# A four-layer graph network on one core: layer 3 counts neighbours block by block, with the later blocks' counts as a row of the masks

## The chip, the cores and the metric

The kernel runs on one core of a Trainium2 chip. Five engines work side by side, each on its own queue of instructions: TensorE (PE: matmuls, with PEld for the weight loads), VectorE (DVE), ScalarE (ACT), GpSimd (POOL) and SyncE (SP, which here only issues DMAs). The metric is the device time of one execution in microseconds (us); lower is better.

## What is computed

Four graph layers follow each other over the same adjacency matrix `adj` (3327 x 3327 float32) and node features `x` (3327 x 64). Each layer's output is added to its input and normalised by row. The change concerns layers 2 and 3.

```python
def _L2_gnn_ref(user_embs, adj, W):
    x = user_embs
    for k in range(2):                     
        agg = adj @ x
        x = jnp.tanh(jnp.concatenate([agg, x], axis=1) @ W[k])
    return x

def _L3_gnn_ref(input, adj, weight, bias):
    support = input @ weight
    mask = (adj != 0).astype(support.dtype)
    rank = jnp.cumsum(mask, axis=1)
    deg = rank[:, -1:]
    k = jnp.minimum(deg, float(MAX_NEIGH))   # MAX_NEIGH = 100, DECAY = 0.5
    pos = rank - (deg - k)
    w = mask * jnp.where(pos > 0, DECAY ** (k - pos), 0.0)
    out = w @ support + bias
    return out
```

So in layer 3 the weight of a neighbour j of a node i is a power of one half whose exponent is the number of i's neighbours after j, and it is zero from the hundredth on. What has to be counted for every pair (i, j) is how many entries of row i of `adj` behind column j are not zero.

## The kernel before

`adj` lies transposed in HBM, padded to 3328 x 3328, so a *block* `jb` is 128 source nodes j (on partitions) by all 3328 target nodes i (on the free axis): 1664 KB of float32. There are 26 blocks. The target nodes are worked in two halves of 1664 (`HALF`), and each half in chunks of 416 (`CW`), four to a half.

**Layer 2** runs in `layers`. For each of two hops (`k`), PE multiplies every block's 128 x 3328 values, in float32, with the 64 features of its nodes: `add(c, jb)` does chunk `c` of both halves at once, each half in 64 output columns (line 421). Hop 1 is `k = 0`, hop 2 is `k = 1`. Seven blocks stay in SBUF throughout (`kept`: four "early" ones, 25 to 22, and three "late" ones, 21 to 19). The others are streamed through buffers: four of the pool `strm` (`UNDER_WAY`) and `MORE` = 2 of the pool `more`, with DMAs issued by SP (line 212) as soon as a buffer is free. The blocks that were streamed last in hop 1 are the first of hop 2 (`ready`). The order of blocks is written out in `order`; the blocks in `end` come last, chunk by chunk (`chunk_end`), each chunk followed by a tanh on ACT.

**Layer 3** works in 52 *steps* `q`: two halves `h`, and in each the blocks from the last to the first. For a step, `masks(q)` loads the half block in float32 (line 339; nothing to load for a kept block) and DVE makes a bf16 mask of zeros and ones from it (line 341). Two PSUM tiles `cnt[0]` and `cnt[1]`, 832 target nodes each, hold the running counts. `count(c, tri, q)` (line 526) adds, by a triangular 128 x 128 matrix `tri`, 100 steps of 128 for the entry itself and minus 128 for each later neighbour in the block; when a step is done, `count(c, rest, q)` adds what `tri` left out, so that the counts of whole blocks stay in PSUM for the following, earlier blocks. `advance(c, q)` does both: `rest` for step q, `tri` for q + 1. `read(c, q, vector)` clamps the counts at zero and writes them as 16-bit integers, whose bits, taken as bf16, are the powers of one half: on ACT (line 541) or DVE (line 539). In the main loop half 0 is read by ACT, half 1 by DVE. `products(q, c)` then multiplies these weights with the features, split in three bf16 parts: two parts in one full-width matmul (line 722), three steps (`LEAD`) behind; the third is collected over `GROUP` = 9 steps and done in one run of half-width matmuls (line 737). The loop over `q` at the end of `layers` writes the order of PE by hand: products of step q - 3, then `advance`, for c = 0 and 1. PE is in program order throughout, as DVE and ACT are in layers 2 and 3. Between the halves (`half_out`) and at the end (`last_out`) the sums are added to the input, normalised and stored.

`with_step` is a list of small operations that are done one per step at the loop's beginning: the bf16 parts of the features of the later groups of nodes.

## Time and profile before

| | |
|---|---|
| runs | 552.27, 552.3, 554.47 us; median 552.3 |
| the profiled execution, its own span | 552.8 us |
| hop 1 of layer 2 | 239.5 to 315.4 us |
| hop 2 of layer 2 | 315.4 to 388.7 us, its last chunks run on into the turn |
| turn from layer 2 to layer 3 | to 407.1 us |
| layer 3's loop | to about 536.7 us |
| last sums, normalisation and stores | to 552.8 us |
| `rest` matmuls | 200, 0.176 us from one to the next |
| `tri` matmuls | 208 |
| DMA in all | 143.56 MB, 260 GB/s over the span |

A profile line of a group names the source line, the engine, the operation, what it writes and reads, the shape and the number of instructions; then its busy time, the mean of one in ns, and the engine's idle time before it with what ended it. A line of the timeline gives start and length in us; successive instructions of one kind are merged, so "0.52 ... x2" are two matmuls that together took 0.52 us from the first's start to the second's end. A matmul's recorded time contains its way through the array, so the distance from one start to the next is the cost of one in a row of them. A float32 matmul appears as two records.

### The profile page before, as it was taken

To read this page: it belongs to the slowest core of one execution; us is meant where nothing else is said; L and a number is where in the kernel's file an instruction comes from. 1 tells how busy PE (TensorE), PEld (TensorE's weight loads), DVE (VectorE), ACT (ScalarE), POOL (GpSimd) and SP (SyncE) were. 2 spreads that over 40 slices of the span, in tenths; PEclk is the share of its full clock that TensorE was granted. 3 is DMA by queue.
4 is the path that set the end of the run, shared out by engine and by line. 5 is a ranking of instruction groups with operands and counts; after the bars stand their busy time and mean duration, and the time that the engine had idled before them with its cause. 6 is when DMAs were issued, how large, how long until landed. Compare 5 with 4: busy or idle time off the path is not lost.

```text
span 552.8 us, 7387 instructions
## 1 busy us (share of the span) xinstructions
PE 524.6 (95%) x2841; PEld 228.6 (41%) x2841; DVE 373.2 (68%) x553; ACT 275.2 (50%) x321; POOL 207.6 (38%) x85
## 2 busy tenths in 40 slices
PE   8879999999999999999999999999999999989991
PEld 5622222222222222854444444444455555645551
DVE  6789999999999999899000011200679769697733
ACT  4699999999999997620000100000365333433321
POOL 3599999999999999000000000000001000000000
PEclk9799999999999999899999999999999999999996
DMA  8979667666777626699999049999019994799601
GB/s 288 341 225 301 219 224 234 212 233 208 232 240 225 209 95 277 247 427 427 421 430 395 3 167 422 429 420 383 32 53 362 323 375 140 238 295 354 244 1 37
DMA packets 33892, 143.56 MB, mean 260 GB/s; under 512 B 10269, under 2 KB 11959, under 8 KB 28855
## 3 DMA queue, kind: packets, MB, share of 16 engines
q1 hardware_dynamic: 31511, 142.40, 69.9%
q10 hardware_dynamic: 2336, 0.59, 0.5%
q8 instruction: 24, 0.39, 0.3%
q14 instruction: 21, 0.17, 0.1%
HBM read 141.53 MB, written 0.87 MB: 258 GB/s over the span
## 4 chain that ended last, share of the span: by engine, by line
PE 66%; DVE 16%; ACT 11%; issue 5%; DVEq 0%; POOL 0%; ACTq 0%; POOLq 0%
PE cnt L421 26%; PE cnt L526 11%; DVE v L1124 8%; PE pq L1103 7%; PE acc L722 6%; ACT pq L1116 5%; ACT sg L1076 5%; PE acc L1133 4%; PE acc L737 3%; DVE a L1115 2%; DVE w L539 1%; DVE mask L341 1%; PE cnt L412 1%; PE idle L928 1%; PE pm L1416 1%
## 5 line engine op out<-in xcount | busy, mean ns | idle before, releaser
L1088 POOL TENSOR_TENSOR sg<-sg,at 128x1664 f32<-128x1664 f32 x44 | 163.9, 3751 | 2.0 <-ACT sg L1076 1.9
L1103 PE MATMUL pq<-riT,ljT 64*128 64x416 f32 x416 | 100.8, 561 | 10.3 <-DVE v L1124 6.2
L1116 ACT ACTIVATE pq<-pq,al,ga 128x832 f32<-128x832 f32 x104 | 104.7, 1011 | 11.0 <-DVE a L1115 11.0
L1124 DVE SCALAR_TENSOR_TENSOR v<-pq,a 128x832 f32<-128x832 f32 x104 | 105.4, 1014 | 3.6 <-ACT pq L1116 2.5
L1115 DVE SCALAR_TENSOR_TENSOR a<-pq,sg 128x832 f32<-128x832 f32 x104 | 105.2, 1012 | 0.5 <-PE prep_fours L1194 0.5
L1133 PE MATMUL acc<-v,xv 128*64 128x416 f32 x416 | 95.3, 537 | 0.0
L1076 ACT ACTIVATE sg<-lb,rb 128x1664 f32<-128x1664 f32 (+1 forms) x53 | 87.2, 1647 | 0.0
L541 ACT ACTIVATE w<-cnt 128x832 int16<-128x832 f32 x55 | 47.2, 862 | 71.2 <-PE cnt L526 71.1
L421 PE MATMUL cnt<-at_l,lj 128*64 128x416 f32 x448 | 80.3, 513 | 0.0
L653 POOL TENSOR_TENSOR s<-sq,s 128x384 bf16<-128x384 f32 (+1 forms) x4 | 4.1, 1024 | 197.9 <-ACT s L652 197.9
L506 ACT ACTIVATE x<-cnt 128x416 f32<-128x416 f32 x8 | 4.1, 517 | 130.6 <-PE cnt L421 130.6
L1103 PEld LDWEIGHTS pq<-riT,ljT 64*128 64x128 f32 x416 | 31.3, 184 | 83.7 <-DVE v L1124 82.8
L539 DVE TENSOR_SCALAR w<-cnt 128x832 int16<-128x832 f32 x49 | 50.1, 1022 | 21.2 <-PE cnt L526 20.8
L526 PE MATMUL cnt<-mask,rest 128*128 128x416 bf16 x200 | 51.5, 339 | 2.4 <-ACT w L541 1.4
L526 PE MATMUL cnt<-mask,tri 128*128 128x416 bf16 x208 | 53.5, 339 | 0.1
L722 PE MATMUL acc<-w,s 128*128 128x416 bf16 x208 | 52.5, 339 | 0.5 <-DVE hid L794 0.5
L421 PEld LDWEIGHTS cnt<-at_l,lj 128*64 128x64 f32 x448 | 31.9, 137 | 46.1 <-issue 45.2
L1133 PEld LDWEIGHTS acc<-v,xv 128*64 128x64 f32 x416 | 20.6, 134 | 61.7 <-issue 58.0
L341 DVE TENSOR_SCALAR mask<-ah 128x1664 bf16<-128x1664 f32 x42 | 43.5, 1035 | 1.0 <-DMA ah<-in_adjT 1.0
L409 DVE COPY lj<-pn_l 128x512 f32<-128x512 f32 (+1 forms) x4 | 2.4, 592 | 60.8 <-PE pn_l L373 60.8
L421 PE MATMUL cnt<-kept,lj 128*64 128x416 f32 x224 | 41.2, 513 | 0.0
L1088 POOL TENSOR_TENSOR sg<-sg,kept 128x1664 f32<-128x1664 f32 (+1 forms) x10 | 30.0, 3026 | 0.8 <-ACT sg L1076 0.8
(291 smaller groups left out, 413.8 us busy)
## 6 DMA issues: line engine op xcount, KB each, us to landing
at_l<-in_adjT SPq DMA_DIRECT2D x24, 1664.0 KB, 12.2
at<-in_adjT SPq DMA_DIRECT2D x44, 832.0 KB, 5.0
ah<-in_adjT SPq DMA_DIRECT2D x42, 832.0 KB, 6.5
bt_l<-in_adjT SPq DMA_DIRECT2D x8, 1664.0 KB, 16.7
kept<-in_adjT SPq DMA_DIRECT2D x7, 1664.0 KB, 9.2
lb<-lf_rows SPq DMA_DIRECT2D x2, 384.0 KB, 6.3
ljT<-ljT SPq DMA_DIRECT2D x4, 128.0 KB, 2.3
x<-in_x ACTq DMA_DIRECT2D x1, 416.0 KB, 5.4
```

The costliest lines, as they stand in the source:

```text
L341: nc.vector.tensor_scalar(mask[q], at, 0.0, None, ALU.not_equal)
L421: nc.tensor.matmul(acc[c][h * D : (h + 1) * D, :], hw[:, slot(jb), :], blocks[jb][:, o : o + CW], start=c not in begun, stop=last, skip_gr ...
L526: nc.tensor.matmul(cnt[c][:, e, :], mat, mask[q][:, of], start=start, stop=(mat is tri), skip_group_check=True,)
L539: nc.vector.tensor_scalar(w.bitcast(I16), cnt[c], 0.0, None, ALU.max)
L722: nc.tensor.matmul(acc[h, c][:, e, :], s12[:, slot(jb)].rearrange("p t d -> p (t d)"), ws[q, c][:, e, :], start=first, stop=last,)
L1076: nc.scalar.activation(sg[:, :, of], lbs[:, :, of], AF.Sigmoid, bias=rb[:, sl : sl + 1])
L1088: nc.gpsimd.tensor_tensor(sg[:, :, of], sg[:, :, of], at[:, :, of], ALU.mult)
L1103: nc.tensor.matmul(pq[:, h, :], ljT[h != jb // NBH][rows, of], riT[rows, ch * CW : (ch + 1) * CW], start=True, stop=True,)
L1115: stt(a_s[t], pqs[t], CUBIC_PLUS, us.pop(t), op0=ALU.add, op1=ALU.mult)
L1116: nc.scalar.activation(pqs[t], pqs[t], AF.Square, bias=al[:, one], scale=ga[:, one])
L1124: stt(w, pqs.pop(t), CUBIC_REST, a_s.pop(t), op0=ALU.add, op1=ALU.mult)
L1133: nc.tensor.matmul(accs[cp, ci][h * D : (h + 1) * D, :], xv[:, slot(jb), :], w[:, h, :], start=(jb == orders[cp][0]), stop=(jb == orders[c ...
```

## The change

Layer 3 no longer carries its counts in PSUM from block to block. Instead the counts of all later blocks are made beforehand, in layer 2: for every block, in bf16 masks of zeros and ones, matmuls against a 128 x 32 matrix of ones and zeros (`upto`) add the block's column sums to the rows of all blocks up to it (`t_masks`, `t_counts`); the four chunks of a half go to four groups of 32 output partitions of one PSUM bank. Nineteen blocks are counted in hop 1, the seven others in hop 2. The result is clamped at 127, and goes to a DRAM tensor `t_rows` of one row per block. In layer 3 each mask's row 0 is overwritten, by a DMA, with the row of its block, and row 0 of `tri` becomes minus 128 throughout, so that one `tri` matmul gives the whole count and `rest` disappears. The first node of each block, whose row was taken, is weighted apart (`first_masks`, `first_weights`), and its products come from `first_rows` and `first_products`.

Nine blocks' masks for layer 3 (`resident`: 25 to 17) are made in hop 2, over the full width, and kept as bf16 where the float32 blocks were; the other 17 blocks are loaded again in both halves. In hop 2 the early kept blocks alternate with the ready ones, and the other kept ones come last. `MORE` goes from 2 to 1, `GROUP` from 9 to 7, and the reads of half 1 go to DVE in odd steps and to ACT in even ones. POOL is put in program order too.

```diff
-MORE = 2
+MORE = 1
+CLAMP = 127.0
+FIRST_T = 8
+BATCH_T = 2
+MASKS = 6
+LOADS = 4
-GROUP = 9
+GROUP = 7
...
+    nc.gpsimd.memset(tri[:1, :], -STEP)
...
-        nc.gpsimd.tensor_copy(tri, tri_f)
-        nc.gpsimd.tensor_scalar(rest, tri_f, -1.0, -STEP, ALU.mult, ALU.add)
...
+        upto = carry.tile([P, 64], BF16, name="upto")
+        nc.gpsimd.memset(upto[:, :32], 1.0)
+        nc.gpsimd.memset(upto[:, 32:], 0.0)
+        tb = carry.tile([P, 2, CW], BF16, name="tb")
+        over = carry.tile([P, NP], BF16, name="over")
+        t_rows = dram.tile([NB + 1, NP], BF16, name="t_rows")
...
+        def first_row(keep):
+            while len(no_row) > keep:
+                q = no_row.pop(0)
+                h, jb = steps[q]
+                half = slice(h * HALF, (h + 1) * HALF)
+                nc.scalar.dma_start(mask[q][:1, :], t_rows[jb + 1 : jb + 2, half])
+        def both_masks(jb, at):
+            nc.vector.tensor_scalar(at, blocks[jb], 0.0, None, ALU.not_equal)
+            resident[jb] = at
...
         def masks(q):
             mask[q] = l3m.tile([P, HALF], BF16, tag="mask", name=f"mask_{h}_{jb}")
-            nc.vector.tensor_scalar(mask[q], at, 0.0, None, ALU.not_equal)
+            nc.vector.tensor_scalar(mask[q], ahead.pop(q), 0.0, None, ALU.not_equal)
+            no_row.append(q)
+            load()
...
+        def t_masks(jb):
+            t_done.add(jb)
+            for h, of in enumerate(halves_of(blocks[jb])):
+                m = t_at.pop(0)
+                t_at.append(m)
+                nc.vector.tensor_scalar(m, of, 0.0, None, ALU.not_equal)
+                t_made.append((jb, h, m))
+        def t_counts():
+            while t_made:
+                jb, h, m = t_made.pop(0)
+                for c in range(CPH):
+                    nc.tensor.matmul(
+                        t_ps[h][c * 32 : (c + 1) * 32, :], upto[:, 31 - jb : 63 - jb],
+                        m[:, c * CW : (c + 1) * CW], start=(h, c) not in t_begun,
+                        stop=len(t_done) == NB, skip_group_check=True,
+                    )
+                    t_begun.add((h, c))
+        def t_out():
+            for h in range(2):
+                nc.vector.tensor_scalar(tb[:, h], t_ps[h], CLAMP, None, ALU.min)
+            for c in range(CPH):
+                nc.gpsimd.dma_start(by_chunk(t_rows)[c], tb[c * 32 : c * 32 + NB + 1])
...
+        def first_weights(m0):
+            nc.vector.tensor_scalar(m0, m0, 0.0, (NEIGH + 1) * STEP, ALU.not_equal, ALU.mult)
+            nc.vector.scalar_tensor_tensor(m0, tb, -STEP, m0, op0=ALU.mult, op1=ALU.add)
+            nc.vector.tensor_scalar(tb.bitcast(I16), m0, 0.0, None, ALU.max)
...
                 if k:
-                    order, others, share = order + others[:5], others[5:], 3
+                    end = [jb for jb in kept if jb not in soon]
+                    for i, jb in enumerate(soon):
+                        order.insert(2 * i + 1, jb)
+                    order += others
+                    place = {
+                        0: [(soon[0], over)],
+                        1: list(zip(soon[1:3], slots_of(soon[0]))),
+                        3: list(zip((soon[3], end[0]), slots_of(soon[1]))),
+                        6: [(order[6], slots_of(soon[2])[0])],
+                        7: list(zip(end[1:], slots_of(soon[3]))),
+                        8: [(order[8], slots_of(soon[2])[1])],
+                    }
...
+                    if jb not in t_done and (k or i >= FIRST_T):
+                        t_masks(jb)
+                        if len(t_made) == len(t_at) or len(t_done) == NB:
+                            t_counts()
+                    if k:
+                        for b, at in place.get(i, ()):
+                            both_masks(b, at)
...
+                    if k and i == 8 + len(t_left):
+                        t_out()
+                        for b, at in resident.items():
+                            nc.gpsimd.dma_start(at[:1, :], t_rows[b + 1 : b + 2, :])
...
+                last_t = [jb for jb in kept if jb not in t_done]
+                for i, jb in enumerate(last_t):
+                    t_masks(jb)
+                    if i % BATCH_T == BATCH_T - 1 and jb != last_t[-1]:
+                        t_counts()
                 for c in range(CPH):
                     chunk_end(c)
+                t_counts()
...
-        def count(c, mat, q, start):
+        def count(c, q):
...
-                    cnt[c][:, e, :], mat, mask[q][:, of], start=start,
-                    stop=(mat is tri), skip_group_check=True,
+                    cnt[c][:, e, :], tri, mask[q][:, of], start=True, stop=True,
+                    skip_group_check=True,
...
-            first = steps[q + 1][1] == NB - 1
-            if not first:
-                count(c, rest, q, False)
-            count(c, tri, q + 1, first)
+            count(c, q + 1)
...
+            if c and jb == 6:
+                first_products(h)
...
+        def first_rows():
+            with nc.allow_non_contiguous_dma(reason="one row of each block"):
+                for cg in range(CPH):
+                    e = cg % 2
+                    for h in range(2):
+                        at = slice(cg * 32 + h * NBH, cg * 32 + (h + 1) * NBH)
+                        nc.gpsimd.dma_start(
+                            sf[at, 0, :], s12[:1, h::2].rearrange("p n t d -> p n (t d)")
+                        )
+                        nc.gpsimd.dma_start(sf[at, 1, e * D : (e + 1) * D], s3[:1, h::2])
+        def first_products(h):
+            for part in range(2):
+                for cg in range(CPH):
+                    of = slice(cg * 32, (cg + 1) * 32)
+                    nc.tensor.matmul(
+                        acc[h, cg // 2][:, cg % 2, :], sf[of, part], tb[of, h],
+                        start=False, stop=False,
+                    )
...
-            lambda: other_parts(C), lambda: first_part(E), lambda: rest_of(E),
-            lambda: other_parts(E), lambda: x3_later(C), lambda: x3_later(E),
+            lambda: (other_parts(C), firsts_weighted()), lambda: first_part(E), lambda: rest_of(E),
+            lambda: (other_parts(E), first_rows()), lambda: x3_later(C), lambda: x3_later(E),
...
+            first_row(1 if to_mask else 0)
             read(0, q, False)
...
-            read(1, q, True)
+            read(1, q, q % 2 == 1)
...
-            masks(q + AHEAD)
+            while consumed and consumed[0] <= q:
+                consumed.pop(0)
+            if to_mask and len(consumed) - len(to_mask) + (m0 is not None) < MASKS:
+                masks(to_mask.pop(0))
```

## The prediction

> **What bounds the kernel now.** I read the page's engine totals first, then the chain of waits, then a table of stages, and last the timelines of the two stages that the change touches.
>
> ```profile
> PE 524.6 (95%) x2841; PEld 228.6 (41%) x2841; DVE 373.2 (68%) x553; ACT 275.2 (50%) x321; POOL 207.6 (38%) x85
> PE cnt L421 26%; PE cnt L526 11%; DVE v L1124 8%; PE pq L1103 7%; PE acc L722 6%; ACT pq L1116 5%; ACT sg L1076 5%; PE acc L1133 4%; PE acc L737 3%; DVE a L1115 2%; DVE w L539 1%; DVE mask L341 1%; PE cnt L412 1%; PE idle L928 1%; PE pm L1416 1%
> ...
> 239.50:315.40 75.90, 75.90 (x426) 31.12 (x425) 21.67 (x43) 1.75 (x4) 0.00 (x0) 1.00 0.85 357
> 315.40:388.70 73.30, 73.30 (x418) 31.51 (x418) 8.16 (x10) 0.52 (x1) 0.00 (x0) 1.00 0.85 349
> 388.70:407.10 18.40, 17.33 (x86) 9.15 (x83) 12.61 (x43) 10.43 (x18) 1.12 (x1) 1.00 0.00 1
> 407.10:536.70 129.60, 127.11 (x812) 70.17 (x811) 100.58 (x113) 48.14 (x61) 2.98 (x3) 1.00 0.71 254
> ```
>
> The last four lines are hop 1 of layer 2, hop 2, the turn to layer 3, and layer 3's loop: length, then busy PE, PEld, DVE, ACT, POOL, the clock, the DMA share, GB/s. PE is busy throughout in three of them. So in these stages a PE instruction taken away is worth its spacing until another wait is longer, and one added costs its spacing at once; DVE and ACT have room. Inside the loop:
>
> ```profile
> 498.58 0.52 PE L722 MATMUL acc<-w,s 128*128 128x416 bf16 x2
> 499.03 3.36 PE L737 MATMUL acc<-w,s 128*64 128x416 bf16 x36
> 502.32 0.53 PE L526 MATMUL cnt<-mask,rest 128*128 128x416 bf16 x2
> 502.68 0.52 PE L526 MATMUL cnt<-mask,tri 128*128 128x416 bf16 x2
> 503.03 0.52 PE L722 MATMUL acc<-w,s 128*128 128x416 bf16 x2
> ...
> 404.62 0.51 PE L526 MATMUL cnt<-mask,rest 128*128 128x416 bf16 x2 [0.25 <-ACT w L541]
> ...
> 412.09 0.51 PE L526 MATMUL cnt<-mask,rest 128*128 128x416 bf16 x2 [0.17 <-DVE w L539]
> ```
>
> A pair of bf16 matmuls is followed by the next after 0.352 us (0.176 each) and is over after 0.52. A step is twice (rest, tri, product): 12 x 0.176 = 2.11 us. Every nine steps come 36 half-width matmuls (L737) in 3.29 us, 0.091 each: two column halves at once. The last two lines show the other limit: PE waiting for the read of its counts, 0.05 us after ACT (0.86 us) or DVE (1.02 us) ends.
>
> Hop 2 streams 13 blocks of 1.70 MB; these are the DMA queue's waits (who, for whom, total, times, longest) and one stretch of the stage table:
>
> ```profile
> SPq L212 <- PE cnt L421: 66.3, 13, 26.9
> ...
> 354.00:360.00 6.00, 6.00 (x36) 2.44 (x34) 0.00 (x0) 0.00 (x0) 0.00 (x0) 1.00 1.01 426
> ```
>
> Every load waits for PE to free a buffer, and then runs at 426 GB/s: 4.0 us a block against 2.79 us of PE. From the first issue (324.43) to the one visible stall (PE weights at 372.3, eleventh block) are 47.9 us: 11 x 4.0 plus some 2 us from issue to landing and 2 us of gaps. So DMA already just keeps up.
>
> **What the Trainium skill says.** "TensorEngine Tiling (Array Packing)", Tiling Modes: with 32 output columns four tiles run independently, and a change of mode drains the array. The trace has the half-width case only: 0.091 us each, and 0.10 us lost at 499.03 on entering it. "TensorE: Matmul & The Clock Gate", Part 3, gives 3.07x for four row tiles and 2.38x for three column tiles. "DMA: Bandwidth & Descriptors", Issuing engines are not separate DMA queues: issuing from another engine saves sequencer time only; the trace shows 0.44 to 0.6 us per issue on SP. "SBUF — State Buffer", SBUF: two separate sides: a DMA issued from GpSimd is held up while VectorE runs a two-port operation; this trace has no such DMA.
>
> **The change part by part.**
>
> *1. Layer 3 loses the `rest` matmuls.* 200 x 0.176 = 35.2 us of PE, of which about 48 steps x 0.704 lie in the loop. What is late next is the loop of count and read: a count's result after 0.52, 0.04 to the reader, 0.86 (ACT) or 1.02 (DVE), 0.05 back: 1.47 or 1.63 us. PE alone needs 8 x 0.176 = 1.41. Half 0 of the counts is always read by ACT, half 1 by DVE in odd steps, so steps alternate at 1.47 and 1.63, mean 1.55; after each burst of L737 (now 28 in 2.56 us, every seven steps) one step runs at 1.41. Saved: 48 x (2.11 - 1.55) = 27 us, plus 0.5: **-27.5 us**. ACT then does three reads of 0.76 (spacing) in two steps, 2.3 of 3.1 us; DVE a read and two masks, 2.9 of 3.1: both fit. Loads fall from 42 to 34 half blocks, 2.0 us each, and run ten ahead: no bound.
>
> *2. Additions in that loop.* Sixteen first-row products: 0.7 us (four row tiles) to 2.8 (one by one): 1.5. `first_weights` puts three DVE operations over 128x832, some 3 us by L539's row, into step 6, ahead of the read of step 7; ACT in steps 3 to 9 also has the casts (0.5 us each). Together +2.4, from 0 to 5. ACT issues 34 row DMAs. At 0.5 us each that is 17 us of ACT's queue; if ACT can issue while it computes, it falls into its waits and costs nothing, which I take; if not, steps on which ACT reads both halves are longer by 0.35: about +7. The row has some 6 us from its issue to its count (three steps), against 2.3 to 5.6 us to landing of small transfers on the page. Sum of part 2: **+3.9**.
>
> *3. The turn.* Two or three `rest` pairs of 0.35 us go from a chain alternating with ACT reads (403 to 407): **-0.9**.
>
> *4. Later blocks' counts in hop 1.* 19 of 26 blocks, two halves each: 38 groups of four 32-column matmuls. Bounds of a group: 0.18 us (all four at once, as the pair of L737) and 0.37 (eight instructions, weights and matmul, at L737's 46 ns each; whether that is PE's limit the trace doesn't say). With the page's 3.07x it would be 0.23. I take 0.19: 7.2 us, plus ten entries into the mode at 0.1: 8.2. DVE makes the masks beside it (idle from 262 to 316, 0.95 us each, four per pair of blocks against 5.6 us of PE): nothing. But at the hop's end blocks 25 and 21 follow directly on the pair before: their four masks (3.8 us) can start only when that pair's counts free the buffers, and PE has nothing else: stall 2.8. **+11.0.**
>
> *5. Hop 2.* From its start (315.4) block order[0] is done after 9.4 us. Before: 22 blocks x 2.79, then three at the end, 8.4: 79.2. After, five blocks are ready, alternating with the early ones, so a stream buffer comes free every 5.6 us instead of 2.8, and there are 14 blocks to load with five buffers. Loads of others 0 to 3 go out at 9, 15, 21 and 26 us. DVE now makes the resident masks, 1.9 us per block: those of 21 and 19 wait for block 22's end (29.0), so 18's is made at 32.8 to 34.7 and only then is its buffer free for block 4. From there loads are back to back: block 4 lands at 40.7, block 13 at 40.7 + 9 x 4.0 = 76.7, and PE ends at 76.7 + 2.8 + 8.4 = 87.9. PE alone (79.2, 14 groups with seven entries 3.4, and 2 us waiting for block 0's masks) would end at 84.6; the loads decide. **+8.5**, from 4 to 13. MORE = 1 costs nothing in hop 1: DMA there ends at 303, 12 us before PE.
>
> *6. POOL's DMAs* (counts out and back, first rows): nothing near waits for them except the first-row products, about 25 us after their 16 issues. Below nothing is excluded, above up to 5 us; I take 0. Fewer constants before layer 2: 0.
>
> Sum: -27.5 + 3.9 - 0.9 + 11.0 + 8.5 = -5.0 from the profiled 552.8: 547.8. The runs' median, 552.3, is 0.5 lower: **547.3**.
>
> **Rivals.**
> *A, slower: the 32-column matmuls don't go four at a time.* Place: PE in both hops. At 0.37 a group, 52 x 0.18 = 9.4 more: 556.7. For it: no 32-column matmul in the trace, and 46 ns an instruction is the fastest there. Against: nothing shows that to be a limit. From 0.28 a group on the change no longer pays.
> *B: ACT's row DMAs block it* (or rows land late): +7, 554.5; the loop's period is then 1.75 instead of 1.55. For it: 0.5 us an issue; against: ACT idles 71.1 us for L526.
> *C: the hop hides more*, loads keep up and no DVE work delays them: -4, and part 2 free, -2.4: 541.
> *D: the change doesn't shorten the step*, because the reads pace it already: part 1 gone, 574.8. L539's 0.15 us waits for PE at every step (its row: 20.8 us idle for PE in all) speak against it.
>
> **How the numbers follow.** Forecast 0.50, with its own range 543 to 551.5; A 0.13, B 0.16, C 0.12, A with B or D 0.09. About 0.5% (2.8 us: below 549.5, above 555.1) is what can be told from no change. Faster: 0.44 of the forecast and C: 0.56. Same: 0.06 of the forecast and half of B: 0.14. Slower: A, half of B and the rest: 0.30. The range takes in C's edge, B and A: 541 to 557.
>
> **What would show it.** No `rest` row, 208 `tri` matmuls, PE waiting for ACT and DVE `w` in each step at a spacing of 1.5 to 1.6 us; the loop near 106 us. A row of 128*32 matmuls with 208 records at under 0.05 us each; a gap of about 3 us before hop 1's last chunks; hop 2 with PE waits for loads of its last two blocks. Wrong if groups take over 0.28 us, if ACT shows DMA issues between its reads with PE waiting, or if PE stands in the first-row products.

## The result and the profile after

The changed kernel takes 558.6 us (median of nine runs, 556.9 to 562.8) beside 553.0 us for the kernel before, a ratio of 1.011 with a 95% interval of 1.008 to 1.014. It is slower by 1.1%; the forecast was 547.3 us and faster. Its profiled execution has a span of 556.9 us, against 552.8.

The page of the changed kernel, with the engine totals and the chain of work that ended last, by engine and by line:

```profile
PE 509.1 (91%) x2865; PEld 209.5 (38%) x2865; DVE 404.1 (73%) x577; ACT 293.6 (53%) x345; POOL 229.6 (41%) x121
PE 17%; DMA 7%; DVE 7%; issue 2%; ACT 2%; DVEq 0%; ACTq 0%
PE cnt L515 6%; DMA ah<-in_adjT 4%; PE cnt L646 4%; DMA at_l<-in_adjT 3%; PE acc L868 3%; PE acc L851 3%; DVE w L659 2%; DVE mask L372 1%; ACT w L661 1%; PE both L722 1%; PE t L452 1%; PE cnt L913 0%; DVE sq L755 0%; DVE tm L445 0%; DVE kept L362 0%
```

PE did lose work (524.6 to 509.1 us busy), yet the span grew. The second line shows DMA in the chain, which had no share in it before. (The chain is followed back over a part of the span only, so the shares don't sum to 100%.) Two loads stand in the third line: `at_l` belongs to hop 2, `ah` to layer 3.

The stages of the changed kernel (length, then busy PE, PEld, DVE, ACT, POOL, granted clock, DMA share, GB/s): hop 1, hop 2, turn, loop.

```profile
237.00:324.90 87.90, 85.57 (x577) 33.75 (x576) 58.11 (x81) 2.09 (x6) 0.19 (x2) 1.00 0.73 309
324.90:413.45 88.55, 80.92 (x486) 32.17 (x482) 34.18 (x30) 0.71 (x2) 10.50 (x19) 1.00 0.74 288
413.45:429.70 16.25, 13.97 (x66) 7.61 (x65) 11.80 (x42) 9.74 (x17) 1.09 (x1) 1.00 0.36 147
429.70:543.30 113.60, 101.62 (x652) 52.14 (x652) 69.68 (x80) 67.61 (x85) 14.95 (x19) 1.00 0.62 231
```

For a fair comparison both kernels are cut at the same events on PE: hop 1 begins with its first product of a block, hop 2 with its first `pn_l` matmul, the turn with the first `both`, the loop with the first `acc`, the end with the last `center` products.

| stage | before, us | after, us | difference | forecast |
|---|---|---|---|---|
| hop 1 | 75.92 | 87.90 | +12.0 | +11.0 |
| hop 2 | 75.28 | 88.55 | +13.3 | +8.5 |
| turn | 16.50 | 16.25 | -0.3 | -0.9 |
| loop | 131.40 | 113.60 | -17.8 | -23.6 |
| end | 14.25 | 13.54 | -0.7 | 0 |

They sum to +6.5. (The prediction's table of stages ends them elsewhere: 73.3 us for hop 2 before and 129.6 for the loop.) The part ahead of hop 1, whose code did not change, was 2.4 us shorter in this one execution, so the spans differ by 4.1; hop 1 began between 237.0 and 239.9 us in all the executions below. The two hops gave away 25.3 us and the loop brought 17.8. The forecast was near in hop 1, and off by 4.8 us in hop 2 and by 5.8 us in the loop.

**Hop 1.** The timeline of PE in the changed kernel (start, us, line, what it writes and reads, shape, count, and in brackets the idle time before it with what ended it), first one batch of counts, then the hop's end:

```profile
265.30 3.01 PE L515 MATMUL cnt<-at_l,lj 128*64 128x416 f32 x16
268.25 0.54 PE L452 MATMUL t<-tm,upto 128*32 128x416 bf16 x8
268.61 0.52 PE L452 MATMUL t<-over,upto 128*32 128x416 bf16 x8
269.06 1.27 PE L515 MATMUL cnt<-at_l,lj 128*64 128x416 f32 x6
...
315.62 0.36 PE L452 MATMUL t<-tm,upto 128*32 128x416 bf16 x4 [0.60 <-DVE tm L445]
316.56 0.36 PE L452 MATMUL t<-tm,upto 128*32 128x416 bf16 x4 [0.57 <-DVE tm L445]
317.49 0.36 PE L452 MATMUL t<-over,upto 128*32 128x416 bf16 x4 [0.58 <-DVE over L445]
318.43 0.36 PE L452 MATMUL t<-over,upto 128*32 128x416 bf16 x4 [0.57 <-DVE over L445]
318.72 5.81 PE L515 MATMUL cnt<-kept,lj 128*64 128x416 f32 x32
```

From 268.25 to 269.06, 16 matmuls with 32 output columns take 0.81 us: 0.36 us for eight, so 0.18 us for a group of four. The section Tiling Modes of the Trainium skill's "TensorEngine Tiling (Array Packing)" has four independent tiles for 32 output columns, and this trace agrees: four take as long as one full-width matmul (0.176 us), and don't go one after the other. At the end PE does a group, waits 0.6 us for the next mask, and so on four times: 2.3 us of waits.

**Hop 2.** PE's timeline at its end, and the stage table of the same stretch:

```profile
388.79 3.01 PE L515 MATMUL cnt<-at_l,lj 128*64 128x416 f32 x16 [0.25 <-DMA at_l<-in_adjT]
393.20 3.01 PE L515 MATMUL cnt<-bt_l,lj 128*64 128x416 f32 x16 [1.40 <-DMA bt_l<-in_adjT]
397.19 3.01 PE L515 MATMUL cnt<-at_l,lj 128*64 128x416 f32 x16 [0.98 <-DMA at_l<-in_adjT]
401.44 3.01 PE L515 MATMUL cnt<-at_l,lj 128*64 128x416 f32 x16 [1.24 <-DMA at_l<-in_adjT]
406.34 3.01 PE L515 MATMUL cnt<-at_l,lj 128*64 128x416 f32 x16 [1.89 <-DMA at_l<-in_adjT]
```

```profile
396.00:400.00 4.00, 3.02 (x18) 1.06 (x16) 0.00 (x0) 0.00 (x0) 3.76 (x8) 1.00 1.01 427
400.00:404.00 4.00, 2.77 (x18) 1.06 (x16) 0.00 (x0) 0.00 (x0) 1.92 (x3) 1.00 0.74 258
404.00:408.00 4.00, 2.11 (x14) 0.77 (x12) 0.00 (x0) 0.00 (x0) 2.06 (x4) 1.00 0.36 100
```

The last five blocks are each waited for. The bracket is only the wait that the profile puts down to the load; from one start to the next are 4.0 to 4.9 us, against 2.8 us of matmuls. The DMA engines are full until 400 us and tail off after it.

**The loop.** Two steps in the steady part, by PE's timeline:

```profile
509.34 0.51 PE L646 MATMUL cnt<-mask,tri 128*128 128x416 bf16 x2
...
510.81 0.51 PE L646 MATMUL cnt<-mask,tri 128*128 128x416 bf16 x2
...
512.50 0.51 PE L646 MATMUL cnt<-mask,tri 128*128 128x416 bf16 x2
...
515.67 0.51 PE L646 MATMUL cnt<-mask,tri 128*128 128x416 bf16 x2
```

From 509.34 to 512.50 and on to 515.67 are two steps each: 3.16 us, so 1.58 a step, against the forecast's 1.55. The steady step is not where the time went. The waits in the loop (who, for whom, us in all, times, longest) tell more:

```profile
ACT w L661 <- DVE mask L372: 11.9, 7, 2.8
...
DVE mask L372 <- DMA ah<-in_adjT: 6.5, 5, 2.4
PE cnt L646 <- DVE w L659: 5.6, 6, 2.3
PE cnt L646 <- ACT w L661: 4.6, 8, 1.4
```

Read upwards from the second: a mask waits for its load, ACT stands behind that mask because the row DMA that ACT has to issue needs it, and PE waits for the reads of both engines. The loads are late in the first half above all. When the loop began, four half blocks had been asked for, and SP asked for the fifth 3.0 us into the loop, when a mask had freed its buffer. Two windows of 6 us, one ahead of the loop and one in its first half:

```profile
424.00:430.00 6.00, 4.29 (x20) 2.47 (x20) 3.83 (x14) 4.54 (x8) 0.00 (x0) 1.00 0.00 0
...
454.00:460.00 6.00, 4.54 (x25) 2.22 (x23) 4.47 (x5) 4.07 (x5) 4.32 (x7) 1.00 1.01 400
```

The DMA engines first stand still and then are full (share 0.00 and 1.01), which the loop's mean share, 0.62, hides.

If one takes 0.176 us for each full-width matmul, 0.091 for each half-width one and 0.0575 for each of the 16 first-row products, and leaves out the normalisation's products between the halves, the gaps that remain between PE's instructions are 5.5 us in the loop of the kernel before and 19.9 in this one. The 190 `rest` matmuls of the loop were 33.4 us of PE; 14.4 us of them came back as gaps.

### The profile page after: what moved, and what is told of

Its sections match the earlier page's. It is cut to its first block, busy times and chain, and to the rows that moved or that the text cites. A ratio compares the mean times of both kernels' runs of the same rounds, so it can differ in the third digit from the quotient of the medians.

```text
span 556.9 us, 7703 instructions
## 1 busy us (share of the span) xinstructions
PE 509.1 (91%) x2865; PEld 209.5 (38%) x2865; DVE 404.1 (73%) x577; ACT 293.6 (53%) x345; POOL 229.6 (41%) x121
## 5 line engine op out<-in xcount | busy, mean ns | idle before, releaser
L1287 DVE SCALAR_TENSOR_TENSOR v<-pq,a 128x832 f32<-128x832 f32 x104 | 105.4, 1014 | 3.2 <-ACT pq L1279 2.2
L515 PE MATMUL cnt<-at_l,lj 128*64 128x416 f32 x496 | 91.4, 515 | 4.3 <-DMA at_l<-in_adjT 4.3
L661 ACT ACTIVATE w<-cnt 128x832 int16<-128x832 f32 x79 | 65.9, 864 | 36.9 <-PE cnt L646 24.2
L464 POOL DMA_DIRECT2D t_rows<-tb x4 | 2.6, 711 | 146.7 <-DVE tb L462 146.7
L515 PEld LDWEIGHTS cnt<-at_l,lj 128*64 128x64 f32 x496 | 34.3, 137 | 55.7 <-issue 48.1
L372 DVE TENSOR_SCALAR mask<-ah 128x1664 bf16<-128x1664 f32 x34 | 35.5, 1057 | 11.0 <-DMA ah<-in_adjT 6.5
L659 DVE TENSOR_SCALAR w<-cnt 128x832 int16<-128x832 f32 x25 | 25.5, 1020 | 20.3 <-PE cnt L646 20.3
L646 PE MATMUL cnt<-mask,tri 128*128 128x416 bf16 x136 | 35.0, 338 | 5.4 <-DVE w L659 2.8
L646 PEld LDWEIGHTS <-tri 128*128 128x128 bf16 x208 | 19.7, 97 | 36.3 <-issue 21.6
L445 DVE TENSOR_SCALAR tm<-at_l 128x1664 bf16<-128x1664 f32 x16 | 15.7, 1023 | 16.8 <-PE t L452 16.8
```

The costliest lines, as they stand in the source:

```text
L372: nc.vector.tensor_scalar(mask[q], ahead.pop(q), 0.0, None, ALU.not_equal)
L515: nc.tensor.matmul(acc[c][h * D : (h + 1) * D, :], hw[:, slot(jb), :], blocks[jb][:, o : o + CW], start=c not in begun, stop=last, skip_gr ...
L646: nc.tensor.matmul(cnt[c][:, e, :], tri, mask[q][:, of], start=True, stop=True, skip_group_check=True,)
L661: nc.scalar.activation(w.bitcast(I16), cnt[c], AF.Relu)
L1287: stt(w, pqs.pop(t), CUBIC_REST, a_s.pop(t), op0=ALU.add, op1=ALU.mult)
```

## The experiments

Each kernel is the changed one with the edit shown, but for `no_rest`. Ratios are against the kernel before, timed on the same chip (medians there 553.6 to 554.9 us), with a 95% interval in brackets. Stage lengths are those of one profiled execution each, cut as above.

One thing in these executions is no part of any edit. In some of them the trace shows PE's granted clock at one half for 3.4 us, behind one or more waits of PE. Where the loop's code and data were those of the changed kernel, it took 113.6 us (the changed kernel) and 113.2 us (`hop1`) without such a stretch, 114.8 and 114.7 us with one (`mask18`, `counts_one`), and 116.3 us with two (`late_pool`). So a difference of over half a microsecond between two loops can be read only after a look at the clock. The executions of the stage table above, before and after, have no such stretch in a stage up to the loop's end.

### Hop 2: what makes the loads late

**late_pool**: counts out to HBM, and back into row 0, at the last streamed block instead of the sixteenth position.

```diff
-                    if k and i == 8 + len(t_left):
+                    if k and i == len(order) - 1:
```

> The later blocks' counts are clamped, written out and read back at the last streamed block of hop 2 instead of seven blocks earlier. Theory 'shared DMA engines': GpSimd's small transfers hold up the tail of the last streamed blocks, so PE's five waits for loads at hop 2's end (6.6 us) shrink to about 2.5 us and the kernel gains 3 to 4 us on the changed one, unless the rows then come too late for layer 3's first count (then the gain reappears as a wait at the turn). Rival 'late start': the waits come only from block 4's load starting 35 us into the hop and 4.0 us a block, so nothing changes (within 1 us).

Measured: ratio 1.010 [1.006, 1.014]. Hop 2 stays at 88.5 us with the same waits for loads, 4.3 and 1.4 us. So GpSimd's small DMAs do not slow the loads. The loop took 116.3 us, with two stretches at half clock; the second alone puts PE 1.5 us further behind the changed kernel's loop.

**mask18**: block 18's resident mask beside 17's, so that DVE makes it before those of blocks 21 and 19.

```diff
-                        6: [(order[6], slots_of(soon[2])[0])],
+                        6: list(zip((order[6], order[8]), slots_of(soon[2]))),
-                        8: [(order[8], slots_of(soon[2])[1])],
```

> Block 18's resident mask is made right after 17's (step 6 of hop 2's order) instead of after those of 21 and 19. Theory 'late start': its stream buffer comes free 2.9 us sooner, block 4 is asked for 3 us sooner, all later loads move up, PE's wait for block 0's masks shrinks from 1.8 us to under 0.5: gain 3 us. Rival 'shared DMA engines': the tail is set by GpSimd's transfers, which move up as well: gain 0 to 1 us at the hop's end.

Ratio 1.008 [1.005, 1.012]; hop 2 takes 85.3 us, 3.3 less. The load that waited for that mask starts earlier, and all behind it come earlier. PE still waits 4.4 us for loads.

**early_loads**: the five ready blocks first, then the four kept ones. Two late streamed blocks, 9 and 10, are kept as masks in place of 17 and 18, and the masks of 19 to 21 are made later.

```diff
-                    for i, jb in enumerate(soon):
-                        order.insert(2 * i + 1, jb)
-                    order += others
+                    order += soon + others
...
```

> Hop 2 takes the five blocks that are in their buffers first and the four kept ones after them, so that a buffer comes free with each 2.8 us of PE rather than each second one; the masks of the two streamed blocks that were kept (17 and 18) are replaced by those of two late ones, so no buffer is held by a mask. Theory (late load starts are hop 2's loss, forecast at 2.5 us and measured at 6.6): hop 2 takes 81 to 83 us for 88.5, and PE waits for loads no more than 2 us in all; the loop stays within 1 us. Rival (the DMA's rate of 4.0 us a block sets the hop, whenever the loads start): hop 2 stays above 85, where the version with 18's mask made earlier came out.

Ratio 1.003 [1.001, 1.005]; hop 2 takes 84.9 us, less gain than expected. A stretch at half clock has part in it: from the start of the last streamed block to the hop's end are 8.8 us here and 7.1 in the changed kernel, so that about 83.2 us would be the order's own (an estimate). PE still waited 0.97 and 1.94 us for the last two loads: the loads started early, filled all five buffers, and then none could start until PE had gone through four kept blocks.

**spread**: two of the kept blocks after the ready ones, one after the sixth and one after the ninth streamed block.

```diff
-                    order += soon + others
+                    order += soon[:2] + others[:6] + soon[2:3] + others[6:9] + soon[3:] + others[9:]
```

> As early_loads, but of the four kept blocks only two follow the five ready ones; the other two stand after the sixth and the ninth streamed block, so that the later loads are not asked for only when PE has gone through all four. Theory (early_loads lost 2.9 us to the last two loads because the DMA engines idled from about 354 to 360 us, all buffers full): hop 2 takes 81.5 to 82.5 us, no wait for a load over 0.5 us. Rival (the loads run at 4.0 us a block against PE's 3.0 to 3.4, so the last ones are late in any order): hop 2 stays above 84.

Ratio 1.000 [0.998, 1.002]; hop 2 takes 81.3 us, 7.3 less than in the changed kernel. All that PE waits for in hop 2 is now (the view of waits, PE alone):

```profile
PE t L452 <- DVE tm L445: 1.5, 2, 0.9
```

No load is in it. The rate of the DMA engines was thus no bound; when the buffers came free was. Two things free them sooner here: the order, and that blocks 17 and 18 no longer hold a buffer until their masks are made. `mask18`, which frees block 18's buffer sooner and changes nothing else, had 3.3 of the 7.3 us; how the rest splits was not tried. The rest of hop 2's price against the kernel before, 6.0 us, is mostly the counts' own: 14 groups with seven entries, 3.2 us by hop 1's figures, and this wait of 1.5; the other 1.3 us were not traced.

### Hop 1: what the counts cost

**counts_one**: only the first block's counts are done; the masks are still made.

```diff
-                for c in range(CPH):
+                for c in range(CPH if (h, CPH - 1) not in t_begun else 0):
                     nc.tensor.matmul(
...
```

> Left out: the count matmuls of all blocks but the first; their masks are still made, at the same places and in the same buffers. It prices the matmuls with their waits. Theory (matmuls and the wait for the last masks make hop 1's 12 us): hop 1 falls from 87.9 to 77.5 to 78.5 us, 36 groups at 0.18, nine entries at 0.09 and 2.3 of waits. Rival (the masks on DVE hold the blocks, so the loads come later, and that is what hop 1 pays): hop 1 stays above 83. In hop 2 theory (loads decide) expects no more than 1.5 us off 88.5, though 14 groups and their entries are 3 us of PE; the rival (PE decides there) expects the whole 3 us.

Ratio 0.994 [0.991, 0.996]. Hop 1 takes 76.5 us, 0.6 above the kernel before: the matmuls and the waits for their masks are the whole of its 12 us, and DVE's masks beside PE are free, as forecast. Hop 2 stays at 89.0 us although 3 us of PE's work are gone from it. PE then waits longer for loads there, 9.7 us: the loads decided.

**hop1**: the last counts go behind the third of the four closing chunks, and block 19's masks are made there.

```diff
-                    t_masks(jb)
-                    if i % BATCH_T == BATCH_T - 1 and jb != last_t[-1]:
-                        t_counts()
+                    if jb != last_t[-1]:
+                        t_masks(jb)
                 for c in range(CPH):
                     chunk_end(c)
+                    if c == CPH - 2:
+                        t_counts()
+                        t_masks(last_t[-1])
                 t_counts()
```

> Hop 1 makes its last counts later: those of blocks 25 and 21 go behind the third of the four last chunks, and block 19's masks are made there, so that DVE has some 3 us of PE's own work to make them in. Theory (PE waited for the masks, because DVE starts them only when the last adds are nearly done): the four waits of 2.3 us go and hop 1 takes 85.5 to 86.0 us for 87.9; the whole 0.3 to 0.4% less than the changed kernel. Rival (the masks are late wherever they are put, the wait moves to the end of the last chunk): hop 1 stays within 0.5 us of 87.9.

Ratio 1.007 [1.005, 1.009]; hop 1 takes 85.1 us, 2.8 less. PE's timeline of that version at the hop's end:

```profile
315.33 0.54 PE L452 MATMUL t<-tm,upto 128*32 128x416 bf16 x8
315.69 0.53 PE L452 MATMUL t<-over,upto 128*32 128x416 bf16 x8
316.15 4.41 PE L515 MATMUL cnt<-kept,lj 128*64 128x416 f32 x24
320.49 0.53 PE L452 MATMUL t<-tm,upto 128*32 128x416 bf16 x8
```

The same counts, no bracket: DVE makes the masks while PE does 12 float32 matmuls of its own (24 records).

### The loop: where 5.8 us are

**no_rest**: the kernel before, without the `rest` products, and with the second read in turn by ACT and DVE.

```diff
-            if not first:
-                count(c, rest, q, False)
-            count(c, tri, q + 1, first)
+            count(c, tri, q + 1, True)
...
-            read(1, q, True)
+            read(1, q, q % 2 == 1)
```

> The kernel before, without the second count product of each step and with the second read in turn by ACT and DVE, as in the changed kernel; nothing else of the change. Left out with the product: what later blocks add to a block's counts. It prices the forecast's first term alone. Theory (the term itself was nearly right): the loop takes 104 to 106 us for 131.4, the span 525 to 527. Rival (steps without the product wait more than forecast, and the loop's 5.8 us are lost here): the loop takes 108 us or more.

Ratio 0.968 [0.966, 0.971]. The loop takes 112.6 us, so this comes out on the rival's side: taking `rest` away is worth 18.8 us here and not 27.5. (A stretch at half clock, 68.5 us into this loop, is at most 1.7 of them, 3.4 us at half; with it taken off, 110.9 us, the side is the same.) DVE's timeline in this version shows why:

```profile
437.32 1.03 DVE L341 TENSOR_SCALAR mask<-ah 128x1664 bf16<-128x1664 f32 x1 [1.01 <-DMA ah<-in_adjT]
438.26 1.02 DVE L539 TENSOR_SCALAR w<-cnt 128x832 int16<-128x832 f32 x1
439.34 1.03 DVE L341 TENSOR_SCALAR mask<-ah 128x1664 bf16<-128x1664 f32 x1
441.36 1.03 DVE L341 TENSOR_SCALAR mask<-ah 128x1664 bf16<-128x1664 f32 x1 [0.99 <-DMA ah<-in_adjT]
```

The masks start at intervals of 2.02 us, the time of one half block's load, and each read stands behind a mask that stands behind its load. Steps had become shorter than loads. This version loads 42 half blocks, the changed kernel 34, so it does not give the changed kernel's own share; the next five do.

**same_loads**: layer 3's loads after the first four are left out, and the masks are made from the four buffers that are there.

```diff
+                if len(loaded) == LOADS:
+                    ahead[q] = loaded[q % LOADS]
+                    return
...
+                loaded.append(ahead[q])
```

> Left out: all loads of half blocks in layer 3 after the first four; every later mask is made from those four tiles, so DMA is nearly idle in the loop and no mask waits for a load. Theory 'loads bound the loop': the loop (113.6 us in the changed kernel) falls by 5 to 6 us, no wait of VectorE for a load and no wait of ScalarE for a mask is left. Rival 'row transfers': the loop is held by ScalarE's issues of 34 rows or by their landing, then it falls by less than 2 us.

**rows_none**: the 34 row DMAs are left out.

```diff
-                nc.scalar.dma_start(mask[q][:1, :], t_rows[jb + 1 : jb + 2, half])
```

> Left out: the 34 one-row transfers into the masks (the masks keep their own row 0). Theory 'loads bound the loop': VectorE still waits for loads, but ScalarE no longer stands behind them: gain 1.5 to 3 us. Rival 'row transfers': gain 5 us or more. If ScalarE's issue costs nothing and the loads alone count: under 1 us.

**both_none** has both of these edits; **no_weights** leaves out DVE's three operations for the first rows' weights (the call in `firsts_weighted`); **bare** leaves out all three things.

> Left out: the loads of layer 3 after the first four and the 34 row DMAs, together; the weights of the first rows are made as in the changed kernel. Each alone left 112.6 us of the loop's 113.6. Theory (a late load makes a late mask, and a late mask holds PE's count and, through the row DMA in ACT's queue, ACT's next read: each cause covers the other): the loop takes 109 to 110 us. Rival (they are 1.0 us each and no more): 111.5 or more.

> Left out: DVE's three operations at the loop's start that turn the counts and the first rows of the matrix into the weights of those rows; loads and row DMAs stay. Theory (most of the 6.5 us by which the bare loop was shorter are these three operations, since loads and row DMAs gave 1.0 each): the loop takes 109 to 110.5 us for 113.6. Rival (each of the three extras is behind the others: taking one away leaves the next in its place): the loop falls by no more than the 2.3 us of the one stall, to 111.3 or more.

> Left out: the loads of layer 3 after the first four, the row DMAs of the 34 streamed masks, and DVE's three operations that turn the counts into the first rows' weights. What is left of the loop is counts, reads, masks and products. Theory (the loop's missing 5.8 us are the change's own extras, DVE's three operations above all): the loop takes 108 to 110 us for 113.6. Rival (the extras cost next to nothing; the steps alternate a little slower than forecast and the loop's start, turn and end have waits of their own that they had before): the loop takes 111 to 112.6, since loads alone left 112.6.

| left out | loop, us | without the half clock | against 113.60 | ratio to before |
|---|---|---|---|---|
| loads | 112.58 | 111.1 | -2.5 | 1.011 [1.008, 1.014] |
| row DMAs | 112.56 | 112.56 | -1.0 | 1.009 [1.005, 1.012] |
| loads and row DMAs | 111.11 | 109.6 | -4.0 | 1.007 [1.004, 1.010] |
| weights' three operations | 111.07 | 111.07 | -2.5 | 1.008 [1.006, 1.011] |
| all three | 107.05 | 107.05 | -6.6 | 0.998 [0.996, 1.000] |

The third column is an estimate in two rows. The loops of `same_loads` and `both_none` contain a stretch at half clock, those of the other three do not. In `both_none` (PE's timeline, and as the last line the stage table's view of 4 us of it):

```profile
444.24 0.51 PE L649 MATMUL cnt<-kept,tri 128*128 128x416 bf16 x2 [2.34 <-DVE w L662]
...
445.78 0.90 PE L649 MATMUL cnt<-mask,tri 128*128 128x416 bf16 x2
446.47 0.90 PE L854 MATMUL acc<-w,s 128*128 128x416 bf16 x2
...
444.00:448.00 4.00, 3.76 (x15) 1.81 (x15) 3.87 (x6) 2.12 (x3) 1.01 (x1) 0.69 0.00 0
```

A pair is followed by the next after 0.69 us, where it is 0.35 elsewhere in this loop, and the granted clock of these 4 us is 0.69, and 0.89 in the 4 us after them: 1.7 us of clock lost, 3.4 us at half. Up to the stretch, PE's instructions in `both_none` start at the same times from the loop's start as in `rows_none`; after it they start 1.5 us later. Beside `bare`, they are 2.4 us late before the stretch (the three operations' stall), 4.0 after it and 4.1 at the end, so nothing later takes the 1.5 us up. In `same_loads` the stretch lies at the same place and costs the same.

No single cause is enough. Loads are worth about 2.5 us, rows 1.0, both together 4.0, which is the 109 to 110 us expected of `both_none`, and the three operations are worth their one stall, 2.5. These 4.0 and 2.5 make the 6.6 us of `bare`. So the three add up, and little of one was hidden behind another. The ratios do not follow the loops: they are those of whole executions, and in the profiled ones of all but `no_weights` a stretch at half clock fell into the end of hop 1 as well, which took 89.1 to 89.6 us for 87.9.

With all gone, PE's waits in the loop are down to (the view of waits for `bare`, where the lines are three higher):

```profile
PE cnt L649 <- ACT w L664: 2.9, 7, 1.4
PE cnt L649 <- DVE w L662: 0.7, 2, 0.4
```

### A version that beats both

**best3** is `spread` and `hop1` together.

> spread and hop1 together. If their gains add: 2.8 us off hop 1 and 6 us off hop 2 against the changed kernel, so about 550 us and 0.6 to 0.8% under the kernel before. If not (the load that hop 1's later end no longer hides): hop 2 above 84 and the whole within 0.3% of the kernel before.

549.95 us, ratio 0.993 [0.991, 0.996]: the two gains add. Hop 1 takes 85.1 us, hop 2 81.3, the loop 114.2. Its masks for layer 3 have less of a lead. By the order of the code, three masks are made ahead of the one being counted in its first streamed steps, where the changed kernel has five, because a streamed block comes two steps sooner.

Three tries at the loop followed. **best4** spreads the three weight operations over the fourth, fifth and seventh of the loop's first steps and makes no mask in those. **best5** is `best3` with the row DMAs on SP's queue (`nc.sync` for `nc.scalar`). **best6** is `best5` with the weights made on GpSimd in four operations.

> best3, and DVE's three operations for the first rows' weights spread over three steps of the loop, with no mask made in those steps, so that no read waits for all three in one go. Theory (the one stall of 2.3 us is their price): 1.5 to 2.5 us less in the loop than best3. Rival (three masks fewer early on, so the streamed masks run late): no gain, waits for masks at 450 to 475 us grow by what the stall gives back.

> spread and hop1 together, and the 34 row DMAs asked for by SP instead of ACT. Theory (ACT's reads wait behind row DMAs whose mask is late; 11.9 us of such waits stand in ACT's list, few of them on the path): the loop gets 1 to 2 us shorter than in the version with ACT. Rival (SP's loads wait for buffers, and rows behind them land later than the count that needs them): the loop gets longer, with PE waiting for rows.

> As best5, and the weights of the first rows are made on the GpSimd engine in four operations instead of on DVE in three. Theory (the stall of 2.3 us, DVE's three operations in front of a read, goes; the engine has till the twentieth step): the loop takes 2 to 2.5 us less than in best5. Rival (GpSimd's four operations take so long, or slow DVE beside them so much, that the masks come late): no gain, and DVE's reads and masks are longer in that stretch than their 0.94 us.

All three fell. `best4`: 1.009 [1.007, 1.012], the loop 124.4 us. In it, by the order of the code, three masks fewer use up the lead, and some streamed steps are counted ahead of their row DMA, so without later blocks' counts. `best5`: 1.006 [1.004, 1.009], the loop 119.5 us, 5.2 longer than in `best3`. PE's waits in that loop:

```profile
PE cnt L651 <- DMA mask<-t_rows: 11.8, 8, 2.6
```

And SP's (L345 is a load, L356 a row):

```profile
SPq L345 <- DVE mask L372: 80.3, 29, 18.4
```

In SP's order each row stands behind a load, and the load waits for the next mask to free its buffer. So the rows land too late, with a lead of three masks; whether they would with a lead of five was not tried. The section Issuing engines are not separate DMA queues of the skill's "DMA: Bandwidth & Descriptors" says that the choice of the issuing engine saves only sequencer time; here it decided 5 us, since what stands ahead in the issuing engine's order comes with the choice. `best6`: 1.013 [1.011, 1.016], the loop 124.5 us. GpSimd's groups in that stretch (busy us, mean ns):

```profile
L481 POOL TENSOR_SCALAR m<-m 128x832 f32<-128x832 f32 x1 | 3.3, 3321 | 0.1
...
L479 POOL TENSOR_SCALAR m<-m 128x832 f32<-128x832 f32 x1 | 3.0, 3020 | 0.1
L480 POOL TENSOR_TENSOR m<-m,tb 128x832 f32<-128x832 f32 x1 | 2.4, 2410 | 0.1
L482 POOL TENSOR_SCALAR tb<-m 128x832 int16<-128x832 f32 x1 | 2.3, 2305 | 0.1
```

11 us instead of DVE's 2.8, and the loop is 5 us longer than in `best5`. PE's waits are only 1.5 us more there; 10.2 us of that loop ran at half clock, worth at most 5.1. What part GpSimd has in it is not shown.

**best7** leaves masks and rows where `best3` has them and does the three operations one by one at steps 15, 16 and 17, where resident blocks leave DVE a gap.

```diff
-            lambda: (other_parts(C), firsts_weighted()), lambda: first_part(E), lambda: rest_of(E),
+            lambda: other_parts(C), lambda: first_part(E), lambda: rest_of(E),
             lambda: (other_parts(E), first_rows()), lambda: x3_later(C), lambda: x3_later(E),
+            *3 * [lambda: None], *(lambda k=k: weights(k) for k in range(3)),
```

> spread and hop1 together, and DVE's three operations for the first rows' weights moved from one place at the loop's start to steps 15, 16 and 17, where no mask is due because the blocks of two steps are resident; masks and row DMAs keep their order. Theory (the three operations in front of one read are a stall of 2.3 us, and there is room for each alone): the loop takes 111.5 to 112.5 us for 114.2. Rival (the sixth mask buffer is held longer, so streamed masks come later): no gain, waits for masks and rows before step 15 grow.

> The same kernel as best3, beside best7 on one chip: 549 to 551 us, 0.5 to 0.9% under the kernel before.

`best7`: 547.5 us (546.6 to 548.6), ratio 0.987 [0.985, 0.989]; `best3` again: 550.0 us, 0.991 [0.989, 0.994]. Its stages, as above:

```profile
237.15:322.25 85.10, 85.10 (x577) 33.52 (x576) 58.22 (x81) 2.09 (x5) 0.19 (x2) 1.00 0.76 319
322.25:403.50 81.25, 79.75 (x486) 32.62 (x482) 34.00 (x30) 0.70 (x2) 12.45 (x19) 1.00 0.79 313
403.50:419.80 16.30, 13.97 (x67) 7.61 (x66) 11.84 (x42) 9.74 (x17) 1.11 (x1) 1.00 0.37 152
419.80:532.10 112.30, 101.98 (x652) 52.09 (x652) 68.28 (x80) 67.26 (x85) 14.72 (x19) 1.00 0.61 234
```

Against the same stages of the changed kernel, PE has as many instructions in the two hops, and is busy throughout hop 1 and but for the 1.5 us in hop 2. The work of the change is all there. What differs is its order, and which two streamed blocks stay resident; the five stages are 11.9 us shorter in all.

## Why the prediction was wrong

*What held.* The steady step, 1.58 us for a forecast 1.55. Groups of four at 0.18 us for 0.19, so rival A fell. Hop 1: +12.0 for +11.0, of which the stall at its end was worth 2.8 us (`hop1`) for a forecast 2.8 (the waits alone are 2.3, so the match to a tenth is luck), and masks on DVE were free (`counts_one`). The turn came within 0.7 us. ACT's row DMAs ran beside its reads, as part 2 had taken it. They took 0.22 us of its queue each, not 0.5: that was read off SP's issues, and "0.44 to 0.6 us" passes over the block loads of layers 2 and 3, which took 0.33 us in the same trace. The first-row products were sized at 1.5 us, and eight of them take 0.46, so about 0.9 for both halves. In hop 2, PE's own work was put at 5.4 us over the kernel before (84.6 less 79.2), and `spread` shows 6.0.

*Part 5, hop 2, was mis-sized by 4.8 us.* (Its own figures, 87.9 less 79.2, give 8.7 and not 8.5.) The mechanism was named: block 18's mask holds a buffer, and the loads decide. Its start was right too: block 4's load was forecast 34.7 us into the hop and asked for at 35.2. The term that failed is "9 x 4.0": block 13 was to land 76.7 us into the hop, and PE began it at 81.4 (406.34 less 324.92). The trace has the DMA engines tailing off in the last 8 us; what makes that tail was not settled, except that it is not GpSimd's DMAs (`late_pool`). With 7.3 us the late loads cost twice the 3.3 that the forecast gave them (87.9 less 84.6).

*Parts 1 and 2, the loop, were mis-sized by 5.8 us together.* The step that failed is "Loads ... run ten ahead: no bound" with "both fit", and the small sum for the additions. The bare loop takes 107.05 us; the forecast for the same content is 131.4 - 27.5 + 1.5 = 105.4. So 1.65 us are the step and its edges. The other 4.1 us lie between the 2.4 that the forecast allowed for additions other than the first-row products and the 6.55 that loads, rows and weights cost together. DVE's three operations were about right (2.5 of the 2.4). The waits for late loads, late masks and the row DMAs behind them had been taken as nothing, and cost 4.0 us together, loads 2.5 and rows 1.0 each alone (the half clock taken off, so estimates). The loads did not run ten ahead in the first half. Four had been asked for when the loop began, the DMA engines stood still before it, and after that a load came every 2.0 us or so against a step of 1.58. The sum behind "both fit", DVE busy for 2.9 of 3.1 us, is an average; one late mask in DVE's order delays the read behind it, and ACT's through the row. `no_rest` shows this at its barest.

*Rivals.* B had a part of it, but for another reason: ACT does not stand for the issue of a DMA but for the mask that it needs. C and D fell. A slower outcome was given 0.30; the mechanism that brought it, loads in both places, stood in the text as a term of the sum and not as a rival.

## What to carry to other kernels

A matmul stream that is taken away had been hiding something. Price the loop without it by the longest of the chains that remain, loads among them, and ask when each load can start and what stands behind it in an engine's order, not how busy the engines are on average. When a hop streams through few buffers, the order of blocks and the masks that hold a buffer set when loads start: 7.3 us were had back by moving blocks that need no load and by making masks of other blocks. Work that waits for another engine's result belongs behind work that does not: 2.8 us in hop 1 and about 2 us in the loop came from moving instructions. And before two single executions are compared to a microsecond, look at the granted clock of the stage in both: 1.5 us of two loops here were the clock's.

## What the hardware showed that was not expected

- Four tiles of 32 columns cost 0.36 us for eight matmuls of 416 columns, half of what the half-width ones take (0.091 each), with some 0.09 us for entering the mode.
- Eight first-row products in 32-row tiles (four at a time) take 0.46 us, 0.0575 each.
- GpSimd needs 2.3 to 3.3 us for an element-wise operation over 128 x 832, where DVE has 1.02 us for its read of the same size (`best6` and the changed kernel).
- A one-row DMA of 3.2 KB issued by ACT takes 0.22 us of its queue, a block's DMA issued by SP 0.33 us.
- PE's granted clock fell to one half for 3.4 us, which cost a loop 1.5 us (`both_none` beside `rows_none`). In five executions this begins within 1.3 us behind the 2.3 us wait for DVE's three operations (`same_loads`, `both_none`, `mask18`, `counts_one`, the second execution of `best3`); in seven others with that wait it does not (the changed kernel, `hop1`, `spread`, `rows_none`, `best3`, `early_loads`, `late_pool`). What sets it off was not tried.
